# Graph attention scores in layer 2: a leaky relu as a linear sum and a relu out of PSUM

## The chip, the core and the metric

The kernel runs on one core of a Trainium2 chip. The metric is the device time of one execution in microseconds (us). The core has TensorE (PE in the profile, its weight loads PEld), VectorE (DVE), ScalarE (ACT), GpSimd (POOL) and SyncE (SP, which issues DMAs). Each engine works through its own queue in order. The matrix products end in PSUM, from which DVE and ACT take them to SBUF.

## The reference

Four layers run one after the other over x of shape (128, 64, 256), that is 128 graphs of 64 nodes with 256 features. Each layer is `x = layernorm(x + f(x))`. Layer 0 has two graph convolutions and four LSTMs over windows, layer 1 a graph convolution with two batch norms, layer 3 a convolution in the eigenbasis of the graph. Layer 2, which the change touches, is a graph attention over 512 edges with 4 heads of 64 features:

```python
Xq = (H @ W_lin.T).reshape(bt, n, h, dh)
Xv = (H @ W_val.T).reshape(bt, n, h, dh)
Qs = Xq[:, src]
Kt = Xq[:, dst]
e = jnp.einsum('behd,hd->beh', jax.nn.leaky_relu(Qs + Kt, LRELU_SLOPE), a)
e = e + jnp.log(A0[src, dst] + EPS)[None, :, None]
...
attn = ex / denom[src]
...
return Y @ W_out.T
```

The slope of the leaky relu is 0.2. The softmax runs over the edges of one source node.

## The kernel before, in words

X, the state, stays in SBUF: 64 tiles of 128 rows, each tile holding the 64 nodes of two graphs. Layer 2 works on pairs of tiles, numbered k from 0 to 31. The generator `scores` (L2147) makes one step per pair; `run` (L2316) draws steps from it and from the other generators that run beside it, and so sets the order of the program. A planner (the tile framework) then orders each engine's queue from the dependencies and its own estimate of times, the earlier instruction in the program first among those that are ready; a few dependencies without a semaphore, made by `after` (L2089), bind the order further.

One step has these parts.

- `transposed(k)` (L2112): four PE transposes bring two tiles of X into one PSUM tile `m`, and DVE copies it to `xT` (L2119).
- `maps(k)` (L2122): PE multiplies `xT` by the weights `wqv` (L2129), one PSUM tile `m` for each of the two tiles of X. ACT copies the first half of the columns to `xq` (L2133) and the second to `xv` (L2143), and `xv` goes out by DMA.
- `edges(c)` (L2160), for two blocks c of 128 features: for each tile i of the pair, PE multiplies `xq` by `GG` (L2166), which has a one for the source and for the target of each of 512 edges. The result, source plus target of every edge, stands in a PSUM tile `l` of two banks, one bank b for each of the two graphs. ACT copies each bank to an SBUF tile `xs` (L2171), and DVE makes it leaky in place as max(0.2 x, x) (L2172).
- `products` (L2094): PE multiplies `xs` by `az`, which holds the attention vector `a` at a shifted place, so that 16 pairs accumulate in one PSUM tile `sc` for each c (L2105). 32 columns of PE work for each of four (b, i) at a time. The 32 pairs form two halves of 16.

PSUM pools: `m` has 2 tiles (pool `l2p`), `l` has 2 tiles of two banks (`l2g`), `sc` has 2 (`l2c`). `m` is shared with the last pass of layer 1, with the softmax and with the values of layer 2. `xs` has 10 buffers, `xq` 4.

Every matrix product in float32 is two PE instructions, so a call of `edges` has 8 (four calls of two), `products` of one c 8, `maps` 8.

What runs beside: in the steps 0 to 14 `last_pass` (L2014), layer 1's last normalization, gives four steps per pair. Two of them transpose a piece back with PE (L2030), add it to X on DVE (L1335) and take statistics (L1338, L1339); the other two prepare the next piece on ACT (L2021) and normalize four tiles at once (`Norm.flush`: L1257 to L1263 on DVE with a square root on ACT at L1259, then L1354 on ACT). In the steps 16 to 21 the softmax of half 0 runs beside (L2202, scans on DVE at L2212 and L2213, exp on ACT at L2221, eight indirect DMAs on POOL at L2252), and in the steps 25 to 31 the values (`mixed`, L2280, PE products at L2289 and L2312, ACT copies at L2269 and L2292). The weights `wqv` stand in the pool `lt`, which lives as long as layer 2; the pool `sx` lives only as long as the scores.

The order of PE in a step comes from the loop at L2176. In the steps with `last_pass` it is edges(0), a step beside, products of (k-1, 1), maps(k+1), a step beside, edges(1), a step beside, products of (k, 0), transposed(k+2), a step beside. In the later steps it is edges(0), maps(k+1), transposed(k+2), edges(1), then the products of (k-1, 1) and (k, 0) together.

Of the kernel before, what the change touches and what calls it, by code (L numbers as in the profile page):

```python
# [1360 lines left out]
def tile_adj_resnorm(ctx: ExitStack, tc: tile.TileContext, I: dict, out: bass.AP, layers: int = 4):  # L1361
    nc = tc.nc
    v, s, te = nc.vector, nc.scalar, nc.tensor
# [10 lines left out]
    for b in range(2):  # L1374
        r, o = slice(b * N, (b + 1) * N), slice((1 - b) * N, (2 - b) * N)
# [9 lines left out]
    X = const.tile([P, NT, D], F32, tag="X", name="X")  # L1385
# [6 lines left out]
    ident = load("ident", [P, P], I["ident"], s)  # L1392
# [219 lines left out]
    with tc.tile_pool(name="lw", bufs=1) as lw, tc.tile_pool(  # L1612
        name="l0c", bufs=1
    ) as lc, tc.tile_pool(name="l0p", bufs=2, space=PSUM) as pp, tc.tile_pool(
        name="l0r", bufs=1, space=PSUM
# [29 lines left out]
        ps = pp.tile([P, 512], F32, tag="ps", name="ps")  # L1645
# [234 lines left out]
    NQ = NT // 4  # L1880
# [172 lines left out]
    with ExitStack() as l2:  # L2053
# [11 lines left out]
        s.dma_start(heads, I["heads"].rearrange("p (h n) -> p h n", n=N)[:, :, 0])  # L2065
        acol = lt.tile([P, 2], F32, tag="acol", name="acol")
        s.dma_start(acol, I["acol"])
        wqv = lt.tile([P, 2, 2 * D], F32, tag="wqv", name="wqv")
        nc.sync.dma_start(wqv, kio(I["WqvT"]))
        wo = lt.tile([P, 2, D], F32, tag="wo", name="wo")  # L2070
        nc.sync.dma_start(wo, kio(I["WoT"]))
# [13 lines left out]
        taken, drawn, last = {}, {}, []  # L2085
        beside = [iter(())]
        soft = []

        def after(ins, those, how=mybir.DependencyClass.Sync):  # L2089
            for i in those:  # L2090
                tc.add_manual_dep(ins.ins, i.ins.name, mybir.DependencyInfo(how, mybir.DependencyReason.DATA),
                                  reason="together")

        def products(todo, held):  # L2094

            xss = [held.pop(x) for x in todo]
            mms = []
            for (k, c), (xs, _) in zip(todo, xss):
                half, u_ = divmod(k, HU)
                if u_ == 0:  # L2100
                    sc[half][c] = pc.tile([P, 512], F32, tag="sc", name="sc")
                for b in range(2):
                    for i in range(2):
                        q = 32 * (2 * b + i)
                        mms.append(te.matmul(sc[half][c][q : q + 32, :], az[:, c, HU - 1 - u_ : 3 * HU - 1 - u_],  # L2105
                                             xs[b, i], start=(u_ == 0), stop=(u_ == HU - 1)))
                if u_ == HU - 1:
                    run(*[soft[half]] * (2 if half and not c else 1))
            after(mms[0], [x for _, ready in xss for x in ready])
            after(mms[0], last[-1:], mybir.DependencyClass.NoSync)  # L2110

        def transposed(k):  # L2112

            ps = pp.tile([P, 512], F32, tag="m", name="m")
            for i in range(2):
                for c in range(2):
                    te.transpose(ps[:, i * D + c * P : i * D + (c + 1) * P], X[:, 2 * k + i, c * P : (c + 1) * P], ident)
            xT = sx.tile([P, 2, 2, P], F32, tag="xT", name="xT", bufs=1)
            v.tensor_copy(xT.rearrange("p i c n -> p (i c n)"), ps)  # L2119
            return xT  # L2120

        def maps(k, xT, apart=False):  # L2122

            xq, xv = [], sx.tile([P, 2, D], F32, tag="xv", name="xv")
            pss = [pp.tile([P, 512], F32, tag="m", name="m") for _ in range(2)]

            def product(i, cols):
                for c in range(2):
                    te.matmul(pss[i][:, cols], xT[:, i, c, :], wqv[:, c, cols], start=(c == 0), stop=(c == 1))  # L2129

            def first(i):
                xq.append(sx.tile([P, D], F32, tag="xq", name="xq", bufs=4))
                drawn[i] = s.copy(xq[i], pss[i][:, :D])  # L2133

            if apart:
                for i in range(2):
                    product(i, slice(0, D))
                    first(i)
            for i in range(2):
                product(i, slice(D, 2 * D) if apart else slice(0, 2 * D))  # L2140
                if not apart:
                    first(i)
                s.copy(xv[:, i, :], pss[i][:, D:])  # L2143
            nc.sync.dma_start(xvd[k], xv)
            return xq

        def scores():  # L2147


            K = NT // 2  # L2150
            xT = transposed(0)
            xq = maps(0, xT, True)
            next(beside[0])
            next(beside[0])
            xT = transposed(1)


            held = {}

            def edges(c):  # L2160
                xs, ready = {}, []
                for i in range(2):
                    pl = pg.tile([P, 2, 512], F32, tag="l", name="l")
                    for b in range(2):
                        r = slice(b * N, (b + 1) * N)
                        mm = te.matmul(pl[:, b, :], xq[i][r, c * P : (c + 1) * P], GG[r, :], start=True, stop=True)  # L2166
                        if not b:
                            after(mm, taken.pop(i, []) + ([drawn[i]] if c == 0 else []))
                    for b in range(2):
                        x = xs[b, i] = sx.tile([P, E], F32, tag="xs", name="xs", bufs=10)  # L2170
                        taken.setdefault(i, []).append(s.copy(x, pl[:, b, :]))  # L2171
                        ready.append(v.scalar_tensor_tensor(x, x, 0.2, x, ALU.mult, ALU.max))  # L2172
                held[k, c] = xs, ready
                last.append(mm)

            for k in range(K):  # L2176
                apart, xn = k < NQ, None
                edges(0)
                if apart:
                    run(*beside)  # L2180
                    if k:
                        products([(k - 1, 1)], held)
                if k < K - 1:
                    xn = maps(k + 1, xT)
                if apart:
                    run(*beside)
                elif k < K - 2:
                    xT = transposed(k + 2)
                edges(1)
                xq = xn  # L2190
                if apart:
                    run(*beside)
                    products([(k, 0)], held)
                    xT = transposed(k + 2)
                    run(*beside)
                else:
                    products([(k - 1, 1), (k, 0)], held)
                if k == K - 1:
                    products([(k, 1)], held)
                yield  # L2200

        def softmax(half):  # L2202
# [113 lines left out]
        def run(*steps):  # L2316
            for x in steps:
                next(x, None)
# [172 lines left out]
```

## Time and profile before

| | us |
|---|---|
| median of three runs (2247.08 to 2248.11) | 2247.27 |
| the profiled execution | 2247.61 |
| its span, first to last instruction | 2245.8 |
| PE busy in the span | 2198.0 |
| DVE busy | 1808.7 |
| ACT busy | 935.1 |
| POOL busy | 162.4 |
| scoring stage, first edge product to last product of scores | 1690 to 2052 |
| DVE, leaky products L2172, 256 operations of 686 ns | 165.3 |
| ACT, copies L2171, 256 operations of 597 ns | 134.1 |
| PE, edge products L2166, 512 instructions | 128.7 |
| PE, maps L2129, 264 instructions | 121.8 |
| POOL, additions L2381 in layer 3, 64 operations of 727 ns | 44.5 |

How to read it: an engine's busy time in a group is the time in which at least one instruction of the group ran on it. Instructions on PE that use different parts of the array run together, and the ends of matmuls are modelled, so the distance from start to start says more than a duration. "Idle before, releaser" gives the time for which an engine stood idle ahead of a group, and the instruction whose end released it. A window gives the busy times of a stretch of the span.

### The profile page before, as it was taken

To read this page: it belongs to the slowest core of one execution; us is meant where nothing else is said; L and a number is where in the kernel's file an instruction comes from. 1 tells how busy PE (TensorE), PEld (TensorE's weight loads), DVE (VectorE), ACT (ScalarE), POOL (GpSimd) and SP (SyncE) were. 2 spreads that over 40 slices of the span, in tenths; PEclk is the share of its full clock that TensorE was granted. 3 is DMA by queue.
4 is the path that set the end of the run, shared out by engine and by line. 5 is a ranking of instruction groups with operands and counts; after the bars stand their busy time and mean duration, and the time that the engine had idled before them with its cause. 6 is when DMAs were issued, how large, how long until landed. Compare 5 with 4: busy or idle time off the path is not lost. (4 is left out here: it accounts for less than half of the span.)

```text
span 2245.8 us, 29967 instructions
## 1 busy us (share of the span) xinstructions
PE 2198.0 (98%) x8810; PEld 1212.1 (54%) x8810; DVE 1808.7 (81%) x9273; ACT 935.1 (42%) x1725; POOL 162.4 (7%) x196
## 2 busy tenths in 40 slices
PE   8999999999999999999999999999999999999997
PEld 6445665445665445665445654554444333446887
DVE  5788887888898899888899998788847777656688
ACT  1432322433322333332333322334437876567675
POOL 0111111111000000000000000000000000100631
PEclk9999999999999999999999999999999999999999
DMA  7001010111010111010111000012210100321522
GB/s 234 22 19 38 1 39 1 38 47 48 1 38 1 38 38 57 1 38 1 38 38 57 1 20 19 20 54 103 75 48 24 38 32 24 88 64 43 154 89 80
DMA packets 44667, 101.55 MB, mean 45 GB/s; under 512 B 5296, under 2 KB 23856, under 8 KB 43216
## 3 DMA queue, kind: packets, MB, share of 16 engines
q1 hardware_dynamic: 38384, 84.64, 11.0%
q0 software_dynamic: 3984, 14.40, 2.3%
q8 instruction: 70, 1.15, 0.2%
q14 instruction: 101, 0.83, 0.1%
q10 hardware_dynamic: 2128, 0.54, 0.1%
HBM read 67.97 MB, written 31.59 MB: 44 GB/s over the span
## 5 line engine op out<-in xcount | busy, mean ns | idle before, releaser
L1725 PE MATMUL pq<-H,wi 128*128 128x512 f32 (+1 forms) x1952 | 781.0, 540 | 1.5 <-ACT gate L1765 1.3
L1765 ACT ACTIVATE gate<-pq,bl 128x512 f32<-128x512 f32 (+1 forms) x504 | 315.8, 632 | 617.8 <-PE pq L1741 503.4
L1725 PEld LDWEIGHTS pq<-H,wi 128*128 128x128 f32 x1952 | 365.5, 190 | 336.9 <-issue 270.3
L1741 PE MATMUL pq<-lh,wh 128*128 128x512 f32 (+1 forms) x1152 | 462.5, 529 | 0.5 <-DVE lh L1783 0.4
L1741 PEld LDWEIGHTS pq<-lh,wh 128*128 128x128 f32 x1152 | 218.8, 190 | 202.8 <-issue 144.1
L2172 DVE SCALAR_TENSOR_TENSOR xs<-xs 128x512 f32<-128x512 f32 x256 | 165.3, 686 | 70.2 <-ACT xs L2171 69.2
L1768 ACT ACTIVATE gate<-lc 128x512 f32<-128x512 f32 (+1 forms) x144 | 83.6, 580 | 277.3 <-DVE lc L1780 111.7
L2171 ACT COPY xs<-l 128x512 f32<-128x512 f32 x256 | 134.1, 597 | 53.8 <-PE l L2166 43.7
L2166 PE MATMUL l<-edge_s,xq 64*128 64x512 f32 x512 | 128.7, 616 | 0.5 <-ACT xs L2171 0.3
L2129 PE MATMUL m<-wqv,xT 128*128 128x512 f32 (+1 forms) x264 | 121.8, 597 | 2.8 <-DVE X L1335 1.9
L1988 PE MATMUL ps<-h,w 128*128 128x512 f32 x256 | 115.1, 608 | 3.3 <-ACT h L1982 3.3
L1354 ACT ACTIVATE X<-X,ln_sh,ln_rs 128x256 f32<-128x256 f32 x187 | 97.5, 592 | 41.5 <-DVE ln_sh L1350 31.1
L1935 PE MATMUL ps<-at,w 128*128 128x512 f32 x256 | 114.1, 597 | 0.1
L796 POOL PARTITION_ALL_REDUCE qQ<-qSG x62 | 74.0, 1193 | 507.9 <-DVE pc L134 258.4
L2129 PEld LDWEIGHTS m<-wqv,xT 128*128 128x128 f32 x264 | 46.4, 189 | 76.6 <-issue 35.8
L1988 PEld LDWEIGHTS ps<-h,w 128*128 128x128 f32 x256 | 49.0, 194 | 63.3 <-issue 53.9
L1935 PEld LDWEIGHTS ps<-at,w 128*128 128x128 f32 x256 | 47.3, 190 | 53.1 <-issue 50.7
L2166 PEld LDWEIGHTS l<-edge_s,xq 64*128 64x128 f32 x512 | 44.5, 186 | 56.9 <-issue 41.7
L1338 DVE BATCH_NORM_STATS2 ln_st<-X 128x6 f32<-128x256 f32 x192 | 73.1, 416 | 1.2
L1783 DVE TENSOR_TENSOR lh<-gate 128x512 f32<-128x512 f32 (+1 forms) x72 | 43.1, 603 | 34.2 <-ACT gate L1765 34.1
L130 DVE SCALAR_TENSOR_TENSOR CS<-GA,qE 64x1 f32<-64x1 f32 x294 | 61.7, 210 | 9.5
L130 DVE SCALAR_TENSOR_TENSOR GA<-qtg,CS,GA 64x1 f32<-64x1 f32 x294 | 61.6, 209 | 8.5
(624 smaller groups left out, 3347.3 us busy)
## 6 DMA issues: line engine op xcount, KB each, us to landing
wi<-in_WihT_dram SPq DMA_DIRECT2D x16, 1024.0 KB, 5.0
wh<-in_WhhT_dram SPq DMA_DIRECT2D x12, 1024.0 KB, 6.6
xd<-X SPq DMA_DIRECT2D x16, 512.0 KB, 2.6
X<-xd SPq DMA_DIRECT2D x16, 512.0 KB, 3.4
xv<-xv SPq DMA_DIRECT2D x32, 256.0 KB, 2.0
xr<-xv POOLq DMA_DIRECT2D x32, 256.0 KB, 3.0
X<-in_x_dram SPq DMA_DIRECT2D x15, 512.0 KB, 8.9
out_dram<-X SPq DMA_DIRECT2D x15, 512.0 KB, 2.9
```

The source lines that it names most:

```text
L130: self.nc.vector.scalar_tensor_tensor(o, a, s, b, op0, op1)
L1354: nc.scalar.activation(x, x, AF.Identity, bias=sh[:, k : k + 1], scale=rs[:, k : k + 1])
L1725: te.matmul(ps, wi[:, kk, o * P : (o + 1) * P], at(kk, k), start=(kk == 0), stop=(k == 0 and kk == 1))
L1741: te.matmul(ahead[gt, c], wh[:, kk, o * P : (o + 1) * P], hst[:, kk, :M], start=False, stop=(kk == 1))
L1765: s.activation(gates[gt][:, c, :M], ps, AF.Tanh if gt == 2 else AF.Sigmoid, bias=bl[:, p - 1, o : o + 1])
L1768: s.activation(*due.pop())
L1935: te.matmul(ps, w1[:, k, c * P : (c + 1) * P], at[:, k, :], start=(k == 0), stop=(k == 1))
L1988: te.matmul(ys[c], w2[:, k, c * P : (c + 1) * P], h[:, k, :], start=(k == 2), stop=(k == 1))
L2129: te.matmul(pss[i][:, cols], xT[:, i, c, :], wqv[:, c, cols], start=(c == 0), stop=(c == 1))
L2166: mm = te.matmul(pl[:, b, :], xq[i][r, c * P : (c + 1) * P], GG[r, :], start=True, stop=True)
L2171: taken.setdefault(i, []).append(s.copy(x, pl[:, b, :]))
L2172: ready.append(v.scalar_tensor_tensor(x, x, 0.2, x, ALU.mult, ALU.max))
```

## The change

With x = source + target, leaky(x) = 0.2 x + 0.8 relu(x). The sum over features of a times 0.2 x is linear, and is the sum of one number for the source and one for the target. So:

- `az` now holds 0.8 a, and `edges` takes relu(x) from PSUM to `xs` in one operation per bank: ACT's relu for graph b = 0, DVE's max with 0 for b = 1. The copies and leaky products are gone.
- After each `maps`, POOL multiplies `xq` by `arow`, the vector a along the free dimension (two operations of 128x256 to `weighed`), and DVE reduces that over the 64 features of a head into `lin` (one operation with 512 inputs per row). `arow` is made once, by two PE products and a DVE copy.
- At the last of 16 pairs of a half, for each c, `linear` multiplies `lin` by 0.2 into the zeroed `linb` (two DVE operations of 64 rows), and PE adds `linb` times `GG` to `sc` (one 128-row product over 512 edges).
- The loop is the same for all steps: edges(0), edges(1), maps(k+1), in the steps with `last_pass` three steps of it, transposed(k+2), one step of it, then both products of the pair together.
- All PE instructions of the scores are tied, without a semaphore, behind the PE instruction that is before them in the program (`chained`, `follow`). The PE instructions of `last_pass`, softmax and values aren't tied themselves.
- `xs` has 8 buffers for 10; `wqv` moves to the pool `sx`.

```diff
-        wqv = lt.tile([P, 2, 2 * D], F32, tag="wqv", name="wqv")
+        wqv = sx.tile([P, 2, 2 * D], F32, tag="wqv", name="wqv", bufs=1)
...
-                v.tensor_tensor(az[:, c, o : o + 1], heads[:, h : h + 1], acol[:, c : c + 1], ALU.mult)
+                v.scalar_tensor_tensor(az[:, c, o : o + 1], heads[:, h : h + 1], 0.8, acol[:, c : c + 1], ALU.mult, ALU.mult)
+        arow = sx.tile([P, D], F32, tag="arow", name="arow", bufs=1)
+        ps = pp.tile([P, 512], F32, tag="m", name="m")
+        for c in range(2):
+            te.matmul(ps[:, c * P : (c + 1) * P], acol[:, c : c + 1].to_broadcast([P, P]), ident, start=True, stop=True)
+        v.tensor_copy(arow, ps[:, :D])
+        lin = sx.tile([P, 2, 2, 2, 2, HU], F32, tag="lin", name="lin", bufs=1)
+        linb = sx.tile([P, 2, 2, 2, 2, HU], F32, tag="linb", name="linb", bufs=1)
+        v.memset(linb, 0.0)
...
+        def chained():
+
+            return [next(i for i in reversed(nc.cur_bb.bb.instructions) if i.engine == te.engine)]
+
+        def follow(ins, those):
+
+            for i in those:
+                tc.add_manual_dep(ins.ins, i.name, mybir.DependencyInfo(
+                    mybir.DependencyClass.NoSync, mybir.DependencyReason.DATA), reason="turn")
+
+        def linear(half, c):
+
+            for b in range(2):
+                r = slice(b * N, (b + 1) * N)
+                v.tensor_scalar(linb[r, c, b], lin[r, half, c], 0.2, None, ALU.mult)
+            turn = chained()
+            follow(te.matmul(sc[half][c], linb[:, c].rearrange("p b i h u -> p (b i h u)"), GG, start=False, stop=False), turn)
...
+                if u_ == HU - 1:
+                    linear(half, c)
                 for b in range(2):
                     for i in range(2):
                         q = 32 * (2 * b + i)
+                        turn = chained()
                         mms.append(te.matmul(sc[half][c][q : q + 32, :], az[:, c, HU - 1 - u_ : 3 * HU - 1 - u_],
                                              xs[b, i], start=(u_ == 0), stop=(u_ == HU - 1)))
+                        follow(mms[-1], turn)
...
             after(mms[0], [x for _, ready in xss for x in ready])
-            after(mms[0], last[-1:], mybir.DependencyClass.NoSync)
...
+            weighed = sx.tile([P, 2, D], F32, tag="weighed", name="weighed")
+            for i in range(2):
+                nc.gpsimd.tensor_tensor(weighed[:, i, :], xq[i], arow, ALU.mult)
+            v.tensor_reduce(lin[:, k // HU, :, :, :, k % HU].rearrange("p c i h -> p i c h"),
+                            weighed.rearrange("p i (c h d) -> p i c h d", c=2, h=2), AX.X, ALU.add)
             nc.sync.dma_start(xvd[k], xv)
...
                     for b in range(2):
-                        x = xs[b, i] = sx.tile([P, E], F32, tag="xs", name="xs", bufs=10)
-                        taken.setdefault(i, []).append(s.copy(x, pl[:, b, :]))
-                        ready.append(v.scalar_tensor_tensor(x, x, 0.2, x, ALU.mult, ALU.max))
+                        x = xs[b, i] = sx.tile([P, E], F32, tag="xs", name="xs", bufs=8)
+                        y = v.tensor_scalar(x, pl[:, b, :], 0.0, None, ALU.max) if b else s.activation(x, pl[:, b, :], AF.Relu)
+                        taken.setdefault(i, []).append(y)
+                        ready.append(y)
...
             for k in range(K):
-                apart, xn = k < NQ, None
                 edges(0)
-                if apart:
+                edges(1)
+                if k < K - 1:
+                    xq = maps(k + 1, xT)
+                if k < NQ:
+                    run(*beside * 3)
+                if k < K - 2:
+                    xT = transposed(k + 2)
+                if k < NQ:
                     run(*beside)
-                    if k:
-                        products([(k - 1, 1)], held)
-                if k < K - 1:
-                    xn = maps(k + 1, xT)
-                if apart:
-                    run(*beside)
-                elif k < K - 2:
-                    xT = transposed(k + 2)
-                edges(1)
-                xq = xn
-                if apart:
-                    run(*beside)
-                    products([(k, 0)], held)
-                    xT = transposed(k + 2)
-                    run(*beside)
-                else:
-                    products([(k - 1, 1), (k, 0)], held)
-                if k == K - 1:
-                    products([(k, 1)], held)
+                products([(k, 0), (k, 1)], held)
                 yield
```

The PE calls of `transposed`, `maps` and `edges` get the same `turn = chained()` and `follow(...)` around them.

More of the change, by code (lines that the diff above doesn't have):

```diff
@@ L2083, in tile_adj_resnorm @@
         xvd = [dl.tile([P, 2, D], F32, tag=f"xv{k}", name=f"xv{k}") for k in range(NT // 2)]
-        taken, drawn, last = {}, {}, []
+        taken, drawn = {}, {}
         beside = [iter(())]
@@ L2116, in transposed @@
                 for c in range(2):
-                    te.transpose(ps[:, i * D + c * P : i * D + (c + 1) * P], X[:, 2 * k + i, c * P : (c + 1) * P], ident)
+                    turn = chained()
+                    follow(te.transpose(ps[:, i * D + c * P : i * D + (c + 1) * P], X[:, 2 * k + i, c * P : (c + 1) * P], ident), turn)
             xT = sx.tile([P, 2, 2, P], F32, tag="xT", name="xT", bufs=1)
@@ L2128, in product @@
                 for c in range(2):
-                    te.matmul(pss[i][:, cols], xT[:, i, c, :], wqv[:, c, cols], start=(c == 0), stop=(c == 1))
+                    turn = chained()
+                    follow(te.matmul(pss[i][:, cols], xT[:, i, c, :], wqv[:, c, cols], start=(c == 0), stop=(c == 1)), turn)
             def first(i):
@@ L2165, in edges @@
                         r = slice(b * N, (b + 1) * N)
+                        turn = chained()
                         mm = te.matmul(pl[:, b, :], xq[i][r, c * P : (c + 1) * P], GG[r, :], start=True, stop=True)
+                        follow(mm, turn)
                         if not b:
@@ L2169, in edges @@
                     for b in range(2):
-                        x = xs[b, i] = sx.tile([P, E], F32, tag="xs", name="xs", bufs=10)
-                        taken.setdefault(i, []).append(s.copy(x, pl[:, b, :]))
-                        ready.append(v.scalar_tensor_tensor(x, x, 0.2, x, ALU.mult, ALU.max))
+                        x = xs[b, i] = sx.tile([P, E], F32, tag="xs", name="xs", bufs=8)
+                        y = v.tensor_scalar(x, pl[:, b, :], 0.0, None, ALU.max) if b else s.activation(x, pl[:, b, :], AF.Relu)
+                        taken.setdefault(i, []).append(y)
+                        ready.append(y)
                 held[k, c] = xs, ready
-                last.append(mm)
             for k in range(K):
-                apart, xn = k < NQ, None
                 edges(0)
-                if apart:
-                    run(*beside)
-                    if k:
-                        products([(k - 1, 1)], held)
-                if k < K - 1:
-                    xn = maps(k + 1, xT)
-                if apart:
-                    run(*beside)
-                elif k < K - 2:
-                    xT = transposed(k + 2)
-                edges(1)
-                xq = xn
-                if apart:
-                    run(*beside)
-                    products([(k, 0)], held)
-                    xT = transposed(k + 2)
-                    run(*beside)
-                else:
-                    products([(k - 1, 1), (k, 0)], held)
-                if k == K - 1:
-                    products([(k, 1)], held)
+                edges(1)
[6 more added lines that the diff above has]
+                if k < NQ:
+                    run(*beside)
+                products([(k, 0), (k, 1)], held)
                 yield
```

## The prediction

> **What bounds the kernel now.** I read the busy times by stretch first. From 1690 to 2052 us of the span the kernel scores layer 2, the only part the change touches. The columns are length, then busy time of PE, weight loads, DVE, ACT, POOL, then the granted clock.
>
> ```profile
> 1690.00:1860.00 170.00, 167.96 (x757) 63.48 (x756) 135.93 (x378) 135.13 (x308) 1.83 (x3) 1.00 0.09 31
> 1860.00:2052.00 192.00, 187.97 (x1060) 79.86 (x1058) 121.80 (x212) 114.94 (x243) 13.80 (x18) 1.00 0.20 57
> ```
>
> PE is busy for 356 of these 362 us; DVE and ACT have about 100 us spare each. So freeing DVE and ACT pays only where PE waits for them. What PE itself does in a step I read from the chain of waits in the quiet second stretch (start, length, what):
>
> ```profile
> 1943.75 1.92 PE l L2166 x8
> 1945.67 1.85 PE sc L2105 x16
> 1947.52 1.92 PE l L2166 x8
> 1949.44 3.63 PE m L2129 x8
> 1953.51 1.92 PE l L2166 x8
> ```
>
> A step is 9.76 us: edges 1.92, products 1.85, edges 1.92, maps with transposes 4.07. And one period of the first stretch, where layer 1's last pass (L2030) runs beside, from the timeline:
>
> ```profile
> 1744.57 0.66 PE L2030 MATMUL m<-ident,y 128*128 128x128 f32 x4
> 1745.16 1.06 PE L2105 MATMUL sc<-xs,az 128*32 128x512 f32 x8
> 1746.15 0.66 PE L2117 MATMUL m<-ident,X 128*128 128x128 f32 x4
> 1746.74 1.99 PE L2166 MATMUL l<-edge_s,xq 64*128 64x512 f32 x8
> 1748.66 0.66 PE L2030 MATMUL m<-ident,y 128*128 128x128 f32 x4
> 1749.24 1.06 PE L2105 MATMUL sc<-xs,az 128*32 128x512 f32 x8
> 1750.24 3.94 PE L2129 MATMUL m<-wqv,xT 128*128 128x512 f32 x8
> 1754.11 1.99 PE L2166 MATMUL l<-edge_s,xq 64*128 64x512 f32 x8
> 1756.03 0.66 PE L2030 MATMUL m<-ident,y 128*128 128x128 f32 x4
> ```
>
> From start to start: 11.46 us = edges 2 x 1.92 + products 2 x 1.00 + maps 3.87 + three transposing groups of 0.59. Maps take 3.53 in a quiet step (start 1928.08, next group 1931.61), so 0.34 here is a wait: the second half's PSUM tile is held until DVE's addition at L1335, which stands among leaky products on DVE.
>
> **What a group of matmuls costs.** Inside an edge group the weight loads start at 1920.49, 1921.03, 1921.46, and the next group at 1922.41: one slot 0.54, one 0.43, two together 0.95. Four slots of 0.43 would be 1.72, the group takes 1.92. So entering and leaving one form of matmul costs 0.20. Products: 1.85 for four slots together, 2 x 1.00 apart. Inside a transposing group starts are 0.11 apart, so one that follows its like takes 0.44 for 0.59.
>
> **Step by step.**
>
> (1) Quiet steps, 16 of them (k from 16 on). Two edge groups become one: minus 0.20. But the second pair's tiles are the first pair's (two PSUM tiles), and its first matmul now follows at once. A drain starts 1.18 after its group:
>
> ```profile
> 1920.49 1.99 PE L2166 MATMUL l<-edge_s,xq 64*128 64x512 f32 x8
> 1921.67 1.07 ACT L2171 COPY xs<-l 128x512 f32<-128x512 f32 x2 [0.86 <-PE l L2166]
> ```
>
> Before, ACT drained both halves (0.54 each in a row). After, ACT takes one with a relu and DVE the other. The relu isn't in this stage; bounds are the copy of that shape, 0.59, and L1698's relu with a scattered output, 1.04; I take the sigmoid's 0.63 (L1765, plain output). DVE's max out of PSUM: bounds 0.66 (L2119's fastest copy out of PSUM) and 0.72 (L2172's slowest), taken 0.68. So the tile is free at 1.18 + 0.68 + 0.05 = 1.91, where the matmul could have gone at 0.54 + 3 x 0.43 = 1.83: a wait of 0.08, and up to 0.10 to start again. Net minus 0.05 per step, bounds minus 0.20 and plus 0.30 (relu at 1.04): **minus 0.8 us**. Products behind them wait for drains done 1.8 us earlier, under the maps.
>
> (2) The first stretch, 15 full steps. Products together: minus 0.15. The maps' wait of 0.34 should go, as DVE loses 8 leaky products of 0.65 and gains 4 drains of 0.68 and a reduction (bounds 0.29, L1447's of 128 columns, and 0.69, any 512-column DVE row; taken 0.68): 1.8 us less in 11.46. ACT loses 4 copies. What is late next: maps and the transposes share two PSUM tiles, and after the change two or three transposing groups stand right behind the maps. The maps' second tile is drained by two copies (0.27 to the next and 0.38), started 0.20 after their end: 0.90 with the semaphore. One transposing group of 0.5 covers it, so 0.35 to 0.40 is waited. The layer-1 transposes aren't tied to a place in PE's order, and the planner has moved such work into a wait before (L2289's at 2049.86, ahead of L2105's last products), so I expect one between the edge pairs, where it covers their wait and keeps their 0.20. Sum: -0.15 - 0.34 - 0.15 (two transposing groups side by side) + 0.38 = -0.26; without moving, -0.6 plus what late drains cost. I take -0.3 x 15 = **minus 4.5 us**; bounds: all 0.97 saved (edges 1.92 + 1.72, maps 3.53, transposes 0.59 + 2 x 0.44, products 1.85 = 10.49), and rival B.
>
> (3) The linear sum adds four matmuls (two per half) of two 128x512 slots each, with entry and exit 0.53 + 0.52: **plus 4.2 us** on PE. Their inputs are a step old and their two DVE products small (0.2); if that cover is gone, 0.4 each. Its first matmuls (L2117-like, 0.6) fall into PE's idle time before 1684: plus 0.3, bounds 0 and 0.6.
>
> (4) PE's two longest waits of the stage come from a full DVE. At 1845.12 the maps waited 1.25 for L1335, behind four leaky products. At 1889.61 a transpose waited 1.97 for a copy on ACT, which stood behind an exp that waited 3.14 for DVE's softmax, itself between leaky products:
>
> ```profile
> 1888.39 0.63 ACT L2221 ACTIVATE se<-se 128x512 f32<-128x512 f32 x1 [3.14 <-DVE se L2214]
> 1889.61 0.66 PE L2117 MATMUL m<-ident,X 128*128 128x128 f32 x4 [1.97 <-ACT xv L2143]
> ```
>
> With half of that DVE work gone I take **minus 2**, bounds 0 and -3.2.
>
> (5) New: a DVE scan of 1.2 us, ACT's table load of 1.28 or its mc copy of 1.09 in front of a drain now stops PE, in the softmax and value steps: **plus 1**, bounds 0 and 3.
>
> (6) No cost: POOL's two multiplies per step. One took 0.727 in layer 3. From xq's copy (0.57 after the maps) 1.46 on POOL and 0.68 on DVE end 2.7 after the maps; the next drain on DVE is due 0.59 + 1.85 + 1.18 = 3.6 after. Eight xs buffers for ten: a tile is written 1.1 us after the products that read it. The weights' other place in SBUF and the memset precede the stage.
>
> POOL beside DVE has a price in rows; these are DVE's small operations of a normalization, in the first stretch and in layer 3, and POOL's multiply there (busy, mean ns):
>
> ```profile
> L1262 DVE SCALAR_TENSOR_TENSOR is_r<-is_r,is_s 128x4 f32<-128x4 f32 x14 | 2.3, 162 | 0.5
> L1262 DVE SCALAR_TENSOR_TENSOR is_r<-is_r,is_s 128x4 f32<-128x4 f32 x24 | 8.7, 362 | 0.4
> L2381 POOL TENSOR_TENSOR X<-X,cb 128x256 f32<-128x256 f32 x64 | 44.5, 727 | 46.5 <-PE ps L2377 29.6 <-ACT X L1354 16.8
> ```
>
> The excess of 0.2 per operation, on 16 normalizations with two such operations, is 6 us of DVE's time and hidden. The Trainium skill, "SBUF — State Buffer", section "Who interferes with whom", says that a DVE instruction with two SBUF inputs is shut out while GpSimd reads SBUF, and one with a PSUM input isn't; the rows agree. L2390, DVE's drain in layer 3 with one input in PSUM, keeps 0.686 beside POOL (L1679's, without POOL: 0.677), so I expect the new drains to stay whole; by row and page alike the sum stays as it is.
>
> Sum: -0.8 - 4.5 + 4.2 + 0.3 - 2 + 1 = -1.8. The profiled execution took 2247.61 (span 2245.8 and 1.8 around it), 0.3 above the median of 2247.27; against the median I forecast **2245.5 us**.
>
> **Rivals.** A, *more is saved*: of (2)'s 0.97 all but the 0.38 for the maps' tile, 0.59 x 15 = 8.9, and of (1) 0.15 x 16 = 2.4: -8.9 - 2.4 + 4.5 - 2 + 0.5 = -8.3, 2239. For it: the change takes load from DVE and ACT, on which the first stretch's chain of waits runs. Against: two tiles in a row with nothing between.
>
> B, *slower: drains queue behind a normalization*. ACT takes four normalizing operations in one piece:
>
> ```profile
> 2010.69 2.08 ACT L1354 ACTIVATE X<-X,ln_sh,ln_rs 128x256 f32<-128x256 f32 x4
> 2012.67 0.35 ACT L2133 COPY xq<-m 128x256 f32<-128x256 f32 x1
> ```
>
> The copy was ready at 2011.1 and came 1.6 later, at no cost then. In front of a drain between the edge pairs it stops PE, and so do addition, statistics and aggregates on DVE (0.69 + 0.75 + 0.30). It decides once a drain is over 0.3 late and nothing is moved in. At 0.9 in 15 steps and 0.65 in the 7 value steps: -1.8 + 13.5 + 4.6 = +16, 2263.
>
> C, *POOL's multiplies behind its eight indirect DMAs* (L2252, 1.02 each, 8.2 in a row), and DVE's reduction, with the drains behind it, waits: 8 once, 2252.
>
> That the relu doesn't replace the leaky product isn't open: L2172's 256 operations are gone from the code.
>
> **Numbers.** Forecast 0.42, A 0.33, B 0.18, C 0.07. Within 0.2% (4.5 us, about what a measurement here can tell from no change): 0.42, of which 0.36 from the forecast, 0.02 from A, 0.04 from C; faster 0.35, 0.31 from A and 0.04 from the forecast; slower 0.23, B's 0.18, 0.03 from C and 0.02 from the forecast. The range reaches to A with (4) in full, (5) and the setup at zero, 2237, and one below for rounding, 2236; upward over C to B at two thirds of its price, 2257.
>
> **What would show it.** L2172 gone; edges as x16 in 3.6 to 4.0 us; products always 1.85; a quiet step 9.6 to 9.9; a first-stretch step 11.0 to 11.4; four calls on sc of 128 rows. Wrong if PE's waits for L2166's drains exceed 5 us in all (B), or if first-stretch steps fall below 10.9 (A).

## The result and the profile after

The changed kernel takes 2327.2 us (median of 4 runs, 2322.5 to 2333.3) where the kernel before takes 2247.7: a ratio of 1.0358, 95% interval 1.0345 to 1.0371. The profiled execution took 2323.7 (span 2321.8). The forecast was 2245.5; the time lies 70 us above its range.

I call *stage* the time from the first edge product's start to the last product's (`sc<-xs`). It was 1689.97 to 2051.53, 361.6 us, and is 1685.79 to 2123.24, 437.4 us: 75.8 us more, nearly the whole loss. Below I compare stages, and not totals alone, because code that the change doesn't touch varies: from 1530 to 1570 the granted clock was 0.91 in the profile before and 1.00 in the one after, and the stage's start lies between 1684.5 and 1691.6 in the profiles of this study.

After, by stretch (length, then busy time of PE, weight loads, DVE, ACT, POOL, then the granted clock):

```profile
1690.00:1860.00 170.00, 133.46 (x579) 52.66 (x578) 87.60 (x244) 86.78 (x194) 16.03 (x22) 0.95 0.05 18
1860.00:2128.00 268.00, 236.26 (x1260) 99.19 (x1258) 125.01 (x249) 108.72 (x228) 44.84 (x62) 0.98 0.17 50
```

DVE and ACT lost the work that they were to lose, and PE now waits: 133 of 170 us busy where it had 168, at a lower clock. Three of the costliest groups of the page (busy, mean ns; idle before, releaser) name the place:

```profile
L2203 PE MATMUL l<-edge_s,xq 64*128 64x512 f32 x512 | 139.1, 653 | 61.9 <-DVE xs L2209 61.9
L2209 DVE TENSOR_SCALAR xs<-l 128x512 f32<-128x512 f32 x128 | 86.7, 689 | 95.7 <-ACT xs L2209 92.8
...
L2209 ACT ACTIVATE xs<-l 128x512 f32<-128x512 f32 x128 | 73.8, 589 | 92.6 <-PE l L2203 91.7
```

Two things are to be seen. PE waits 61.9 us for DVE's drains of the edge tiles. And DVE, before its drains, waits 92.8 us for **ACT's drain**: the two banks of a tile aren't emptied side by side. In a quiet step of the timeline:

```profile
1961.36 1.99 PE L2203 MATMUL l<-edge_s,xq 64*128 64x512 f32 x8
1963.96 1.99 PE L2203 MATMUL l<-edge_s,xq 64*128 64x512 f32 x8 [0.62 <-DVE xs L2209]
1965.88 3.70 PE L2160 MATMUL m<-wqv,xT 128*128 128x512 f32 x8
```

The second pair follows 2.60 behind the first, where the forecast had 1.91, and a quiet step takes 10.45 us for 9.76. In the first stretch it is worse. One step there, all engines, only the rows that matter:

```profile
1743.98 1.99 PE L2203 MATMUL l<-edge_s,xq 64*128 64x512 f32 x8
...
1745.51 0.58 ACT L2209 ACTIVATE xs<-l 128x512 f32<-128x512 f32 x1
...
1746.53 0.68 DVE L2209 TENSOR_SCALAR xs<-l 128x512 f32<-128x512 f32 x1
1746.65 2.07 ACT L1354 ACTIVATE X<-X,ln_sh,ln_rs 128x256 f32<-128x256 f32 x4 [0.56 <-DVE ln_sh L1350]
...
1747.27 1.13 PE L2203 MATMUL l<-edge_s,xq 64*128 64x512 f32 x4 [1.31 <-DVE xs L2209]
1748.63 1.05 ACT L2209 ACTIVATE xs<-l 128x512 f32<-128x512 f32 x2
1749.24 1.29 DVE L2209 TENSOR_SCALAR xs<-l 128x512 f32<-128x512 f32 x2 [2.02 <-ACT xs L2209]
...
1749.98 1.81 PE L2203 MATMUL l<-edge_s,xq 64*128 64x512 f32 x4 [1.58 <-DVE xs L2209]
1751.72 4.67 PE L2160 MATMUL m<-wqv,xT 128*128 128x512 f32 x8
```

The first tile's max (1746.53) stands behind layer 1's small operations on DVE; PE waits 1.31. The second tile's relu (1748.63) stands behind four normalizing operations on ACT; DVE was free from 1747.2, but waits 2.02 for that relu, and PE waits 1.58 more. Then the maps take 4.67 instead of 3.70: PE itself is slower after the waits, for its granted clock (third number from the end) is 0.50 for 3.41 us:

```profile
1750.30:1753.71 3.41, 3.41 (x7) 0.96 (x4) 0.92 (x2) 0.60 (x1) 0.00 (x0) 0.50 0.00 0
```

Steps 2 to 13 (counted from 0) all have the same waits, but only six of them have such a slow piece. These take 16.0 to 16.1 us, the other six 14.4, where the kernel before took 11.46.

The first 16 steps cost 56.8 us more than before, the rest of the stage 19. Of the 19, 5.2 lie in step 23, which e15 explains, and 5.9 in step 16, where the softmax begins. There the max of a drain stands behind a scan of the softmax on DVE, and PE has its longest wait of the stage:

```profile
1928.35 1.22 DVE L2239 TENSOR_TENSOR_SCAN sf<-edge_s,sf 128x512 f32<-128x512 f32 x1
...
1930.22 0.68 DVE L2209 TENSOR_SCALAR xs<-l 128x512 f32<-128x512 f32 x1
...
1930.96 3.58 PE L2203 MATMUL l<-edge_s,xq 64*128 64x512 f32 x8 [4.26 <-DVE xs L2209]
```

### The profile page after: what moved, and what is told of

It reads as the page before. It is cut to its first block, busy times and chain, and to the rows that moved or that the text cites. A ratio compares the mean times of both kernels' runs of the same rounds, so it can differ in the third digit from the quotient of the medians.

```text
span 2321.8 us, 29940 instructions
## 1 busy us (share of the span) xinstructions
PE 2211.3 (95%) x8822; PEld 1220.2 (53%) x8822; DVE 1765.9 (76%) x9187; ACT 879.0 (38%) x1597; POOL 208.1 (9%) x260
## 5 line engine op out<-in xcount | busy, mean ns | idle before, releaser
L1765 ACT ACTIVATE gate<-pq,bl 128x512 f32<-128x512 f32 (+1 forms) x504 | 315.5, 632 | 618.4 <-PE pq L1741 503.9
L1725 PEld LDWEIGHTS pq<-H,wi 128*128 128x128 f32 x1952 | 365.8, 190 | 337.5 <-issue 270.9
L2203 PE MATMUL l<-edge_s,xq 64*128 64x512 f32 x512 | 139.1, 653 | 61.9 <-DVE xs L2209 61.9
L2209 DVE TENSOR_SCALAR xs<-l 128x512 f32<-128x512 f32 x128 | 86.7, 689 | 95.7 <-ACT xs L2209 92.8
L2209 ACT ACTIVATE xs<-l 128x512 f32<-128x512 f32 x128 | 73.8, 589 | 92.6 <-PE l L2203 91.7
L2177 POOL TENSOR_TENSOR weighed<-xq,arow 128x256 f32<-128x256 f32 x64 | 46.5, 727 | 476.0 <-ACT xq L2164 476.0
L1335 DVE TENSOR_TENSOR X<-m,X 128x512 f32<-128x512 f32 x38 | 25.8, 678 | 62.8 <-PE m L2030 46.9
```

The lines of the kernel that those rows point to most:

```text
L1725: te.matmul(ps, wi[:, kk, o * P : (o + 1) * P], at(kk, k), start=(kk == 0), stop=(k == 0 and kk == 1))
L1765: s.activation(gates[gt][:, c, :M], ps, AF.Tanh if gt == 2 else AF.Sigmoid, bias=bl[:, p - 1, o : o + 1])
L2209: y = v.tensor_scalar(x, pl[:, b, :], 0.0, None, ALU.max) if b else s.activation(x, pl[:, b, :], AF.Relu)
```

## The experiments

All of them. Each ratio is to runs of the kernel before on the same chip; the chips differ from row to row, so ratios and stages compare better than medians. "Step" is the usual step of the first stretch. e7 leaves out the linear sum, e13, e16 and e17 leave out the normalization, and e4 counts the linear part twice, so these don't compute the whole model; what matters is their amount of work.

| run | median us | ratio, 95% interval | stage | step |
|---|---|---|---|---|
| before | 2246 to 2250 | 1 | 361.6 | 11.46 |
| after | 2327.2 | 1.0358 [1.0345, 1.0371] | 437.4 | 14.43, 16.09 |
| e1 own banks | 2287.5 | 1.0176 [1.0159, 1.0193] | 399.7 | 12.57 |
| e2 old order | 2252.5 | 1.0011 [1.0001, 1.0020] | 365.8 | 11.22 |
| e3 both | 2254.9 | 1.0023 [1.0010, 1.0035] | 365.8 | 11.22 |
| e4 old drains | 2342.6 | 1.0405 [1.0381, 1.0428] | 461.7 | 17.07 |
| e16 no norm | 2279.6 | 1.0137 [1.0122, 1.0153] | 392.7 | 11.90 |
| e13 own banks, no norm | 2267.2 | 1.0076 [1.0061, 1.0092] | 379.7 | 11.40 |
| e17 joined, no norm | 2239.2 | 0.9971 [0.9958, 0.9984] | 356.1 | 10.74 |
| e6 one between | 2330.7 | 1.0366 [1.0351, 1.0381] | 439.6 | 14.45, 16.09 |
| e11 the same, own banks | 2281.8 | 1.0152 [1.0137, 1.0167] | 393.0 | 12.30 |
| e5 fill | 2322.8 | 1.0333 [1.0318, 1.0349] | 433.8 | 14.44 |
| e7 no linear sum | 2245.1 | 0.9976 [0.9964, 0.9987] | 355.0 | 11.22 |
| e12 late sum | 2328.0 | 1.0356 [1.0336, 1.0376] | 442.2 | 14.43, 16.09 |
| e15 DVE product | 2322.2 | 1.0322 [1.0303, 1.0341] | 434.8 | 14.50, 16.15 |
| e8 joined | 2248.3 | 0.9986 [0.9976, 0.9996] | 358.4 | 10.88 |
| e9 before, joined | 2247.2 | 0.9995 [0.9986, 1.0004] | 360.6 | 11.48 |
| e10 joined, late sum | 2248.1 | 0.9997 [0.9987, 1.0008] | 360.0 | 10.88 |
| e14 joined, DVE product | 2245.4 | 0.9980 [0.9970, 0.9990] | 354.1 | 10.88 |
| e18 the same, own banks | 2255.6 | 1.0034 [1.0024, 1.0044] | 367.8 | 11.70 |

My theories after the result: **S**, the drains of a tile stand in series because ACT and DVE read one PSUM tile; **O**, the new order leaves no work between the edge groups, so that a late drain stops PE.

### e1: a PSUM tile for each bank

```diff
-                    pl = pg.tile([P, 2, 512], F32, tag="l", name="l")
+                    pl = [pg.tile([P, 512], F32, tag="l", name="l", bufs=4) for _ in range(2)]
```

> The changed kernel with each half (bank) of an edge product in a PSUM tile of its own, four tiles instead of two of two banks; order and arithmetic as in the changed kernel. In its trace DVE's max starts 0.03 us after the end of ACT's relu of the same tile, so a tile is drained in 0.60 + 0.69 us one after the other. Theory S (the drains stand in series within a tile): side by side a tile is free 0.60 us sooner. The quiet step falls from 10.45 to about 9.8, and of the 80 us that the change cost most go: 2250 to 2270 us. Theory O (order: both edge groups follow at once, and in the first stretch nothing of the other work stands between them, so that their drains queue behind layer 1's normalization on ACT and DVE): the quiet step falls the same, some 10 to 15 us in all, but the first stretch keeps steps of 13.5 or more where before had 11.46: 2300 to 2320 us.

Half goes, 40 us, which lies between the ranges of the two theories. DVE's 92.8 us of waiting for ACT's drains are gone from the list of waits; in a quiet step the two run together, and it takes 9.95:

```profile
1907.28 0.60 ACT L2209 ACTIVATE xs<-l 128x512 f32<-128x512 f32 x1 [2.70 <-PE l L2203]
...
1907.34 1.48 DVE L2209 TENSOR_SCALAR xs<-l 128x512 f32<-128x512 f32 x2 [1.50 <-PE l L2203]
```

The Trainium skill, "PSUM — Partial Sum Buffer", section "Specifications (TRN2)", says that ScalarE and VectorE can access PSUM in parallel at full rate unless they collide on a bank. These rows agree. In the changed kernel too each engine has banks of its own; only the tiles differ, so what kept the two apart was a wait in the program that goes by the tile, not the chip. The first stretch keeps 12.57:

```profile
1748.95 1.99 PE L2203 MATMUL l<-edge_s,xq 64*128 64x512 f32 x8
1750.17 0.60 ACT L2209 ACTIVATE xs<-l 128x512 f32<-128x512 f32 x1 [2.18 <-PE l L2203]
1750.66 0.20 ACT L1259 ACTIVATE is_s<-is_t 128x4 f32<-128x4 f32 x1
1750.89 0.18 DVE L1260 RECIPROCAL is_r<-is_s 128x4 f32<-128x4 f32 x1 [0.55 <-ACT is_s L1259]
...
1751.18 0.68 DVE L2209 TENSOR_SCALAR xs<-l 128x512 f32<-128x512 f32 x1
...
1752.01 2.21 PE L2203 MATMUL l<-edge_s,xq 64*128 64x512 f32 x8 [1.08 <-DVE is_r L1262]
```

DVE's reciprocal waits for ACT's root, the root stands behind a relu, and the max stands behind the reciprocal. (The last row names L1262, but the tile depends on the max, which ended at 1751.86.) So S isn't all.

### e2 and e3: the old order, with shared and with own banks

```diff
                 edges(0)
+                if apart:
+                    run(*beside)
+                    if k:
+                        products([(k - 1, 1)], held)
+                if k < K - 1:
+                    xn = maps(k + 1, xT)
...
                 edges(1)
```

> The changed kernel's arithmetic (relu and max straight from PSUM, linear sum, GpSimd's products, tied order of PE's instructions) in the loop order of the kernel before: maps, layer 1's transposes and the earlier pair's products stand between the two edge groups. The drains of a tile are still in series (0.60 + 0.69 us). Theory O: the order was what cost, so nearly all goes: first stretch 11.0 to 11.7 a step, total 2245 to 2262 us. Theory S: a tile in series is late in any order: over 2290 us, with waits of PE's edge products for DVE's max of 50 us or more in the stage.

> Both: the old loop order and a PSUM tile for each bank. Theory O: within 5 us of the run with the old order alone, since other work covers 1.3 us of drain there. Theory S: 30 us or more below it. Both theories: no tile is waited for, so 2240 to 2255 us: 2247 + 4 for the linear sum, less what a lighter DVE saves (2 to 7).

Both came out as theory O said. DVE still waits 52.8 us for ACT's drains in e2, and PE only 4.0 us in the stage for DVE's: with other work between the edge groups the series costs next to nothing, and own banks add nothing (e3). The order turned a harmless lateness into 75 us. e2, e3 and the runs built on their order also go back to ten `xs` buffers, but the eight were not what PE waited for: in the changed kernel's trace no drain (L2209) waits for a product to free a buffer, only for the edge products and for the other engine's drain.

### e4: the old drains in the new order

```diff
-                        y = v.tensor_scalar(x, pl[:, b, :], 0.0, None, ALU.max) if b else s.activation(x, pl[:, b, :], AF.Relu)
+                        taken.setdefault(i, []).append(s.copy(x, pl[:, b, :]))
+                        ready.append(v.scalar_tensor_tensor(x, x, 0.2, x, ALU.mult, ALU.max))
```

> The changed kernel's order, with linear sum and GpSimd's part, but with the drains of the kernel before: ACT copies both halves out of PSUM, DVE makes the leaky part in SBUF. The scores therefore count the linear part twice and weigh the leaky part by 0.8; the amount of work is what matters. DVE gets back 256 operations of 0.69 us and ACT twice 0.57 in series per tile. Theory O: the order alone costs, so about as slow as the changed kernel or slower, 2310 to 2350 us. Theory S (DVE waiting for ACT at a drain is the loss): a tile free after 2 x 0.57 without DVE, 2250 to 2290 us.

O again: 15 us slower than the changed kernel. But PE waits no longer there, 0.65 and 1.98 us in a step for 1.31 and 1.58; what is longer is PE's own work, at a clock of 0.86 from 1700 to 1800 for 0.95. So the one-operation drain isn't what costs; whether it helps in this order isn't shown, because the clock differs.

### e13, e16 and e17: without the normalization beside the scores

```diff
-                    ln.flush()
+                    ln.todo = []
```

> The changed kernel with a PSUM tile for each bank, and without the normalization that layer 1's last pass runs beside the scores (four ACT operations of 0.52 us, ACT's root and DVE's six small operations every other half step are left out, so the scores see unnormalized nodes). With own banks alone the first stretch took 12.57 us a step, of which PE waited 1.08 for a max queued behind these operations and 0.36 for the maps' tile, and the old order 11.22. Theory B (the queue behind the normalization is what own banks leave): 11.1 to 11.6 us a step, 2264 to 2272 us. Rival (what is left is the missing distance between the two edge groups, with or without a queue): 12.2 us or more a step, 2280 to 2288 us.

> The changed kernel, banks shared as they are, without that normalization (same work left out). Theory S and B as two causes that add up: the drains stay in series (0.60 + 0.69 us), the first stretch keeps the quiet step's wait of 0.62 us and takes 11.8 to 12.6 us a step: 2275 to 2290 us. If B alone makes the first stretch slow: about 11.3 us a step as with own banks, 2264 to 2272 us. If S alone: over 13.5 us a step, 2310 us or more.

Together with e1 a table of two causes, in us of stage: 437.4 with both, 399.7 without the shared tile, 392.7 without the normalization, 379.7 without either. Alone, the shared tile costs 13.0 and the queue behind the normalization 20.0; together 57.7, that is 24.7 more than the sum. One reason is in the rows of the changed kernel: a series hands on what delays its first member, so ACT's 2.07 us of normalization delays the relu, and through it DVE's max. Another is the clock: six steps of the changed kernel are some 1.65 longer by it, 10 us in all, while from 1700 to 1800 it is 1.00 in e1, e13 and e16. How much of the 24.7 is which isn't shown. Both step expectations held (11.40; 11.90, and there the quiet step's wait of 0.62). Of the 18.1 us that e13's stage is still above before, 4.2 are the linear matmuls, about 5 the step of 15.41 that e15 explains and 6.5 step 16 (16.37 for 9.89); the rest is not taken apart further.

> Control for the two runs without normalization: the joined order with edges apart, GpSimd making the products, and the normalization of layer 1's last pass left out as there. In this order PE is busy throughout, so if those two runs became faster because drains no longer stood in a queue, and not because there is less work, nothing is gained here: first stretch 10.8 to 10.9 us a step, 2245 to 2249 us. Rival (less work on ACT and DVE is worth something by itself): 2240 us or less.

The total, 2239.2, is in the rival's range. But the kernel before was also 2.7 faster beside these runs than beside e8's: by the ratios the two are 3.4 us apart, with intervals that overlap, and by the stage the control gains 2.3 us, 0.14 a step. So some 2 of the 20 us come from less work and not from the queue; the reading stands.

### e6 and e11: one yield of layer 1's pass between the edge groups

```diff
                 edges(0)
+                if k < NQ:
+                    run(*beside)
                 edges(1)
...
-                    run(*beside * 3)
+                    run(*beside * 2)
```

> The changed kernel with one of the yields of layer 1's last pass (in every other place a transposing group of 0.59 us, in the others its normalization) put between the two edge groups of the first stretch, as the prediction had expected of the planner. If the prediction's reading is right that one group there covers the wait, the first stretch falls to some 12 us a step, about 35 us less: 2285 to 2295 us. If what is late is the drains themselves, in series and behind layer 1's operations on ACT and DVE, 0.59 us of other work covers 0.59 of 2.9 us of wait at most: 2312 to 2327 us.

> The same with a PSUM tile for each bank. The run with own banks alone kept a wait of 1.08 us a step in the first stretch, for a max on DVE that stands behind layer 1's small operations, themselves waiting for ACT. If that queue is what is left (theory O with rival B's mechanism), one group between covers about 0.6 us a step or moves the small operations away from the drains: 2274 to 2283 us. If the series within a tile was all, nothing is left to cover: 2285 to 2290 us as with own banks alone.

In e6 the 0.65 of transposes now lie between, and the first wait behind them grows from 1.31 to 2.42 (the second falls from 1.58 to 0.33; together 2.89 and 2.75). ACT's four normalizing operations, which stood between two drains, now stand in front of the first one, and DVE, done with the addition that follows the transposes, waits 0.93 for that relu:

```profile
1752.56 2.07 ACT L1354 ACTIVATE X<-X,ln_sh,ln_rs 128x256 f32<-128x256 f32 x4 [1.04 <-DVE ln_sh L1350]
...
1753.52 0.69 DVE L1335 TENSOR_TENSOR X<-m,X 128x512 f32<-128x512 f32 x1 [1.00 <-PE m L2030]
...
1754.54 0.57 ACT L2209 ACTIVATE xs<-l 128x512 f32<-128x512 f32 x1
...
1755.15 0.69 DVE L2209 TENSOR_SCALAR xs<-l 128x512 f32<-128x512 f32 x1 [0.93 <-ACT xs L2209]
...
1755.89 1.13 PE L2203 MATMUL l<-edge_s,xq 64*128 64x512 f32 x4 [2.41 <-DVE xs L2209]
```

Nothing is covered; the step is unchanged, and the total lies above both ranges. With own banks the group between is worth 0.27 a step, and the total (2281.8) lies in the first range. What covers the drains in e2 is much longer than one layer-1 group: the maps alone are 3.7 us of PE.

### e5: filling the waits

```diff
+                    if c and k < NQ:
+                        fill = pp.tile([P, 512], F32, tag="m", name="m")
+                        for b in range(2):
+                            turn = chained()
+                            follow(te.matmul(fill, xq[i][:N, :P], GG[:N, :], start=True, stop=True), turn)
```

> The changed kernel, with two extra 64-row, 512-column matmuls (0.43 us each, result not used) on TensorE ahead of each tile of the second edge group in the first stretch, where TensorE waits 1.31 and 1.58 us: 64 of them with 0.9 us in each wait. In the changed kernel every other step has matmuls after the second wait that start 0.73 to 1.01 us apart instead of 0.43 to 0.54, and the step is 16.09 instead of 14.43 us, at a granted clock of 0.95. Theory C (TensorE runs slower because of the idle time): with the waits filled the alternation goes and the stretch takes 14.4 us a step throughout, 8 to 20 us less in all: 2307 to 2320 us. Rival (the slow matmuls have another cause, such as a transfer or GpSimd at work): no gain, 2325 to 2335 us, steps of 16.09 remain.

More work, less time: the windows of after and of e5 from 1700 to 1800.

```profile
1700.00:1800.00 100.00, 77.40 (x332) 30.37 (x329) 50.31 (x141) 49.97 (x112) 8.75 (x12) 0.95 0.04 16
```

```profile
1700.00:1800.00 100.00, 96.42 (x404) 41.63 (x396) 51.44 (x146) 51.54 (x117) 9.49 (x13) 1.00 0.04 16
```

The clock is 1.00 again and of the first 16 steps all but the first two and the last two take 14.44. So idle time slows PE, as theory C has it. The total fell by 4.4 only, against 8 to 20 expected, and the two ratios' intervals overlap: PE wasn't slow in every other step throughout (6 of 16 in the changed kernel), and the steps at the ends stay long. What shows the cause is the steps and the clock, not the total. The Trainium skill, "TensorE: Matmul & The Clock Gate", section "HAM oscillation — how this bites in real kernels", gives gaps of over about 3.4 us as the danger. Here two gaps of 1.31 and 1.58 us a step were enough for 0.95, so by that figure alone the loss would have been missed.

### e7, e12, e15 and e14: what the linear sum costs

e7 leaves `linear` and the products behind it out of e2; e12 issues the reduction of one step behind the next step's products; e15 and e14 change one word, in the changed kernel and in the joined order (e8):

```diff
-                nc.gpsimd.tensor_tensor(weighed[:, i, :], xq[i], arow, ALU.mult)
+                v.tensor_tensor(weighed[:, i, :], xq[i], arow, ALU.mult)
```

> The run with the old order, without the linear sum: GpSimd's multiplications, DVE's reductions, the small scaling and the four linear matmuls are left out, so the scores lack their linear part. The prediction priced it at 4.2 us (four matmuls of 1.05) plus 0.4 at most for each late input. If that holds: 4 to 6 us below the run with the old order, 2246.5 to 2249 us. Rival (the two-operand drains and the softmax behind them cost something too): within 2 us of that run.

The sum costs 7.4 us of the total and 10.8 of the stage, not 4.2. Its matmuls are as priced (1861.65 to 1862.70 in e2: 1.05). Nearly all of the rest lies in steps 22, 23 and 28: 12.10, 11.44 and 16.68 for 9.87, 9.76 and 14.64. In the changed kernel the same place is one step of 14.97:

```profile
2010.72 1.40 POOL L2177 TENSOR_TENSOR weighed<-xq,arow 128x256 f32<-128x256 f32 x2
...
2012.16 0.69 DVE L2178 TENSOR_REDUCE lin<-weighed 128x8 f32<-128x512 f32 x1 [5.36 <-POOL weighed L2177]
...
2013.50 3.48 PE L2203 MATMUL l<-edge_s,xq 64*128 64x512 f32 x8 [3.65 <-DVE xs L2209]
```

POOL's multiplications stand behind eight indirect DMAs, DVE's reduction waits 5.36 for them, the max stands behind the reduction, PE waits 3.65 and then takes 3.48 for a group of 1.99.

> The changed kernel with DVE's reduction of a step's weighed products issued one step later, so that it finds GpSimd's result ready. In the changed kernel one reduction waited 5.36 us because GpSimd's multiplications stood behind eight indirect DMAs of the softmax; the max of an edge tile stood behind it on DVE, TensorE waited 3.65 us and then ran the group in 3.48 instead of 1.99 us. Rival C's mechanism at work: 4 to 6 us less, 2321 to 2323 us. If the wait only moves (the reduction is not what holds DVE): within 2 us, 2325 to 2329 us.

Inconclusive: in the trace the reduction still stands in its old place, and it still waits up to 5.6 us for POOL.

> The changed kernel with the weighed products on DVE instead of GpSimd (0.35 to 0.45 us each on DVE, two a step), so that no DVE reduction can wait for a GpSimd that is at its indirect DMAs. Rival C's mechanism (one wait of 3.65 us and a slow edge group behind it, the step of 14.97 us): that step falls to 10.5 to 11.5 us; if nothing else changes 2322 to 2325 us. Against it: 0.8 us more of DVE a step delays the drains of the first stretch, 15 x 0.3 to 0.8 us: 2328 to 2340 us, with the long step gone all the same.

The long step falls from 14.97 to 10.55, for 0.07 more in a first-stretch step, the stage by 2.6 and the total by 5.0. PE's wait in that step falls from 3.65 to 0.72. Rival C's mechanism is shown.

> The joined order with edges apart, and the weighed products on DVE. Issuing the reduction one step later in the program did not move it on DVE: it still waited for GpSimd, 3.9 us at the longest, and PE 2.2. Without GpSimd in the chain the linear sum should cost its four matmuls only: the steps 22, 23 and 28 fall from 12.1, 11.4 and 15.0 or 16.7 to about 9.9, 9.8 and 14.7 as without the linear sum; 3 to 4 us below the joined order, 2243 to 2246 us. Rival (DVE's extra 0.8 us a step is on the path): 2248 us or more.

As expected: steps 22, 23 and 28 are 9.87, 9.76 and 14.64, the stage 4.3 us shorter than e8's.

### e8, e9, e10 and e18: the change in an order that suits it

```diff
                 edges(0)
+                if apart:
+                    run(*beside)
+                if k < K - 1:
+                    xn = maps(k + 1, xT)
...
                 edges(1)
                 xq = xn
+                products(([(k - 1, 1)] if k else []) + [(k, 0)], held)
+                if apart:
+                    run(*beside)
+                    xT = transposed(k + 2)
+                    run(*beside)
```

> The changed kernel's arithmetic with the two edge groups apart, but with the products joined in the first stretch as well: edges, layer 1's transposes, maps, edges, both products (of the earlier second pair and of the first pair), transposes. Theory O: a drain has 4.2 us of other work on one side and 2.9 us on the other, so no tile is waited for; the joined products and neighbouring transposes save 0.2 to 0.35 of the 11.22 us per step of the run with the old order: 2247 to 2250 us. Theory S: waits of PE for DVE's max of some 0.3 us a step: 2252 to 2258 us.

> The arithmetic of the kernel before (ACT copies, DVE makes the leaky part, no linear sum) in the same joined order. If what the change can gain lies in the order of TensorE's groups and not in the drains: 0.2 to 0.35 us a step, 2243 to 2247 us. If a DVE that carries all leaky products can't follow: 2247 us or more, with the maps still waiting 0.3 us a step for the addition of layer 1.

e8 came out as theory O said: 10.88 a step. With the arithmetic of before the same order gains nothing (11.48): PE waits 7.3 us for the addition L1335 on DVE, which carries the leaky products. So here the joined products pay only with the lighter drains.

> The joined order with edges apart, and the late reduction. The linear sum should then cost its four matmuls of 1.05 us alone, without GpSimd's queue: 3 us below the joined order, 2243 to 2246 us (by the stage, 355 to 356 us from the first edge group to the last product, where the kernel before takes 361.6). Rival: the reduction was hidden there, 2247 to 2249 us.

The rival's range: nothing gained, for e12's reason (the reduction waits up to 3.9 us for POOL). e14 is the fastest kernel with the whole computation, 0.2% below before (0.9980, 0.9970 to 0.9990). Its stage is 7.5 us shorter than before, its total 3.9: from the last product to the end it takes 198.5 us for 194.3. Every run here took 197 us or more there, e9 with the arithmetic of before too; why stays open.

> The joined order with DVE's products, and a PSUM tile for each bank in addition. With other work between the edge groups no tile is waited for (0.6 us in the whole stage), so the series within a tile costs nothing: within 2 us of the joined order with DVE's products, 2243 to 2247 us. Rival (shared tiles still cost, spread thin): 2 us or more below it, 2243 us or less.

Neither: own banks cost 10 us there, 13.7 of the stage. One drain on DVE now stands in front of layer 1's addition where it stood behind it in e14, and PE's maps wait 0.7 us for the addition 15 times (10.3 us).

## Why the prediction was wrong, point by point

- **The step that failed**, in (1): "ACT takes one with a relu and DVE the other ... So the tile is free at 1.18 + 0.68 + 0.05 = 1.91". The durations were right (0.60 and 0.69), though the 0.63 taken for the relu was a mean of two shapes (L1765 at 128x512 alone: 0.683); that they lie side by side was assumed and not asked. In series the second pair follows 2.60 behind the first, and a quiet step became 0.69 longer, not 0.05 shorter. The code gave reason to ask: both banks are slices of one tile.
- **The second**, in (2): "I expect one between the edge pairs, where it covers their wait". The planner left the groups in program order, and e6 shows that one there would have covered nothing. PE waited 2.9 us a step for drains that stood behind layer 1's normalization on ACT and DVE, and at times ran at a clock of 0.50 after these waits. The -4.5 for 15 steps became +52.8, which contains some of (1). Its small terms held: products 1.86, neighbouring transposes 0.49 to 0.53, the maps' wait for L1335 gone, and the wait for the maps' tile 0.35 for 0.38.
- **Rival B** named the right mechanism and priced it at 18 us (13.5 + 4.6). It has 20 us of stage alone and 45 together with the series (437.4 less 392.7). It was priced as one wait; through the shared tile a delay of ACT becomes one of DVE, and twice a step. Its sign of being wrong, more than 5 us of PE waits for the drains, came with 61.9.
- **(3)** 4 x 1.05 held. The missing term was rival C's, about 4 to 6 us, of which the prediction gave 7% odds and 8 us.
- **(4)** held: the waits of 1.25 and 1.97 are gone. **(5)**, plus 1 with 3 at most, was too low: the one wait of step 16 behind the softmax is 4.26 us, and the step 5.9 longer than before. **(6)** "No cost" was wrong in the one place where POOL has something else to do, and eight buffers for ten were not tried apart from the order, but no drain is seen to wait for one.
- What the forecast believed in exists: in e14 a first-stretch step is 0.58 below before, more than the -0.3 taken. It needs the other order.

## What to carry to other kernels

Before pricing two engines as draining one tile side by side, see whether the program lets them: if the wait goes by the tile, count the sum, or try a tile for each (worth 40 us in this order, a loss of 10 in the joined one). And distance between a producer and the reuse of its buffer is worth more than fewer switches: here 0.2 us saved per joined group was paid with up to 2.9 us of waiting, because the order had been what hid late drains. What fills the distance must be long enough and must not bring other work in front of the drains (e6), and keep what a busy queue delays (POOL at its DMAs) out of the queue that drains.

## What the runs showed of the hardware

- Idle gaps of 1.31 and 1.58 us in each step of 14.4 us brought the granted clock to 0.95 from 1700 to 1800, and gaps of 0.65 and 1.98 us brought it to 0.86 (e4). It was 0.50 for 3.41 us after some of the gaps and not after others, with matmuls 0.73 to 1.01 us apart instead of 0.43; two useless matmuls in each gap brought it back to 1.00 (e5). Gaps of 1.08 and 0.35 us a step left it at 1.00 (e1).
- ACT and DVE read two PSUM banks at the same time at their usual 0.60 and 0.69 us each (e1).
- A product of 128x256 took 0.73 us on POOL and 0.43 on DVE.
